# A perceiver layer on one core: the first pair's loads, its key normalisation and two other steps are rearranged

## The chip, the cores and the metric

The kernel runs on one core of one Trainium2 chip. The core has five engines with an instruction stream each: TensorE (PE in the profile, with its weight loads as PEld), VectorE (DVE), ScalarE (ACT), GpSimd (POOL) and SyncE (SP). An engine works its stream off in order. Transfers are issued by instructions in the streams of SP, ACT or POOL. The metric is the device time of one execution in microseconds (us); three executions of the kernel before gave 618.97, 621.19 and 622.3, with a median of 621.19.

## The reference

The inputs are 32 batches of latents `x` (64 x 128), of a context (1601 x 128) and of a mask over the context, which is true for the last 0 to 400 positions of a batch. One layer is computed:

```
ln  = layernorm(layernorm(x)) * g_l + b_l             # latents, 64 rows of a batch
xn  = layernorm(ctx) * g_x + b_x                      # context
q   = ln @ Wq;   k, v = split(concat(xn, ln) @ Wkv)   # 16 heads of 64
out = softmax(mask(q k^T)) v                          # a context position counts where its mask is true
x   = x + layernorm(out @ Wout) * g_o + b_o
x   = x + self_attention(layernorm(x))                # 16 heads of 8, a distance term in the scores
x   = x + quantised_ffn(layernorm(x))                 # 128 -> 352 -> 128, fake quantisation to 8 bits
```

Only those last positions count, so a batch is worked with between 72 and 464 keys, its 64 latents among them.

## The kernel before

The batches are ranked by how many context positions they need; `order` holds the ranking and `CAPS` the number of positions that each rank may need. Batches are worked in 16 pairs (`PAIRS`): the two halves of the 128 partitions are the latents of the two batches. The first pair is small: ranks 31 and 17, with 8 and 192 context positions, in one tile and two tiles of 128 partitions.

**Weights.** Queries and keys are never formed by themselves. `a_sb` holds Wq Wk^T per head (made by `turn_weight`, which transposes four 128 x 128 blocks on TensorE and copies the bank out, and by `head_products`, four matmuls a bank, evacuated on ScalarE at line 287). So the queries of a pair are `lnT` times `a_sb` (`queries`, lines 801 and 805) and the keys are the normalised context itself, transposed (`keys_T`, lines 787 and 791). `b_sb` holds Wv Wout per head in the same way, and is made inside the main part by `late_constants`.

**Two parts with a branch between.** The prologue loads the mask and Wq on SP and the key half of Wkv on ACT, ranks the batches on VectorE (lines 168 to 193), loads the latents of the first pair (line 207) and makes `a_sb`. Then every engine reads `arm` (line 1258) and branches (line 1312) to one of three bodies of `attention`; the first has the capacities of `CAPS`, and is the one that runs. The order inside the body's start is written by hand (`tc.manual_schedule`): on SP the loads of the first pair's context and mask (`load`, lines 670 to 689), the value half of Wkv and Wout (lines 1224 and 1225), then the latents, context and mask of the second pair; on the other engines `latents(0)`, `latents_T(0)`, `measure` and `prepare` for the two batches, `queries` in four quarters with `keys_T` between.

**Normalising.** `latents` takes mean and variance with bn_stats and bn_aggr on VectorE, the power -0.5 on POOL (`rstd_of`, line 703), and then three VectorE steps: line 951 (subtract the mean, times rstd), 710 (times g), 711 (plus b). For the context, `measure` does the statistics (lines 729, 730, 699, 703), and `prepare` a small `shift` on VectorE (739), one ScalarE instruction a tile (743), two VectorE steps for g and b (237, 238), a copy of the latents into the key tile on POOL (748) and the mask terms on POOL (754).

**The main loop.** Then 128 steps (16 pairs, 8 steps of two heads each). In each step `logits` does the score matmul (833), a VectorE scan that adds the mask terms and finds the lowest value (836) and the exponential on ScalarE (841); one to four steps later the probabilities are transposed (881, 890, 896) and multiplied with the keys (916, 927), scaled by VectorE (933), and projected (961). The work of other pairs is put between by a table of steps: statistics and keys of pair t+1, loads of pair t+2, projection, self attention and FFN of the pairs before. Within the stretch between scheduling barriers the framework's scheduler may reorder an engine's instructions, so the written order is not all. In the body's first steps, `late_constants(0)` (transposes of the value weights, lines 256 and 257) stands at step 1, and products of `b_sb` at steps 2 and 3.

## Time and profile before

| what | us |
|---|---|
| median of three executions (618.97 to 622.3) | 621.19 |
| the profiled execution | 618.87 |
| its span, from the first instruction to the last | 617.2 |
| PE busy in the span | 583.2 |
| DVE, ACT, POOL busy | 444.8, 409.2, 130.4 |
| branch reached: `arm` written on VectorE | 11.47 |
| last evacuation of `a_sb` on ScalarE ends | 14.69 |
| transposed latents `lnT` ready | 17.42 |
| first score matmul starts | 25.49 |

The span is counted from the first instruction; the 1.67 us between the span and the profiled time lie around it. Four views of the profile carry what follows. The page gives busy time by engine. The table of stretches gives busy time and the clock that was granted to TensorE. The timeline lists instructions in order of time, merged where equal ones follow each other, with start, duration, engine, line, tiles, shape, and in brackets how long the engine was idle before and what it waited for. The view of one source line also shows instructions of an engine's sequencer (a name that ends in q): branches, register loads, and waits.

### The profile page before, as it was taken

What the parts mean: (1) busy time and instruction counts of PE and PEld (TensorE: products, weight loads), DVE (VectorE), ACT (ScalarE), POOL (GpSimd) and SP (SyncE); (2) the same over time, 40 slices, a digit from 0 to 9 for tenths busy, and PEclk for the clock granted to TensorE, in tenths of its full rate; (3) what the DMA queues carried; (4) which work ended last, traced back from release to release, by engine and by line L of the source; (5) the groups of instructions that cost most, each with busy time, mean ns of one, the idle gap of its engine ahead of it and who ended that gap; (6) DMA issues with size and microseconds to landing.
All of it is one profiled execution on the core that took longest, in us unless ns stands there. A gap on an engine that the chain in (4) does not pass through costs nothing. (4 is left out here: it accounts for less than half of the span.)

```text
span 617.2 us, 14248 instructions
## 1 busy us (share of the span) xinstructions
PE 583.2 (94%) x4758; PEld 470.9 (76%) x4758; DVE 444.8 (72%) x1674; ACT 409.2 (66%) x1107; POOL 130.4 (21%) x320
## 2 busy tenths in 40 slices
PE   4799899999999999899999989999999999999993
PEld 4687768868896878788787878778788979777473
DVE  5578566777869676787867587786858694778983
ACT  3587476667667665676856666675767686685692
POOL 2431120424132341212120130312021211010102
PEclk9899999999999999999999999999999999999997
DMA  4433312021222112031311213011312311110002
GB/s 101 108 67 87 92 19 59 25 62 22 53 42 49 40 18 64 20 71 27 63 22 40 44 34 67 27 53 20 53 36 40 46 36 36 35 35 20 0 21 55
DMA packets 39285, 27.93 MB, mean 45 GB/s; under 512 B 18223, under 2 KB 30515, under 8 KB 39203
## 3 DMA queue, kind: packets, MB, share of 16 engines
q1 hardware_dynamic: 38755, 26.14, 20.3%
q8 instruction: 40, 0.66, 0.5%
q10 hardware_dynamic: 224, 0.56, 0.3%
q14 instruction: 42, 0.34, 0.3%
q0 software_dynamic: 224, 0.23, 0.2%
HBM read 25.73 MB, written 1.18 MB: 44 GB/s over the span
## 5 line engine op out<-in xcount | busy, mean ns | idle before, releaser
L841 ACT ACTIVATE s<-s,low 128x464 f32<-128x464 f32 (+22 forms) x256 | 133.5, 523 | 87.0 <-DVE low L836 69.5
L833 PE MATMUL bank_s<-xT,qT 128*128 128x464 f32 (+22 forms) x512 | 147.2, 406 | 4.7 <-DVE low L836 4.4
L916 PE MATMUL bank_m<-pT,xn 128*128 128x256 f32 (+10 forms) x560 | 145.0, 384 | 0.0
L916 PEld LDWEIGHTS bank_m<-pT,xn 128*128 128x128 f32 (+10 forms) x560 | 104.4, 191 | 43.1 <-issue 22.6
L703 POOL TENSOR_TENSOR rstd<-rstd,mhalf 128x1 f32<-128x1 f32 (+3 forms) x96 | 59.2, 623 | 329.5 <-DVE rstd L699 322.3
L836 DVE CUSTOM_DVE_ANT_0 s<-bank_s,ad 128x464 f32<-128x464 f32 (+22 forms) x256 | 107.3, 432 | 11.2 <-PE bank_s L833 10.3
L833 PEld LDWEIGHTS bank_s<-xT,qT 128*128 128x128 f32 x512 | 77.9, 193 | 13.4 <-DVE low L836 8.0
L933 DVE TENSOR_TENSOR oT<-bank_m,rden 128x256 f32<-128x256 f32 x128 | 77.2, 614 | 7.4 <-PE bank_m L927 2.7
L801 PE MATMUL bank_m<-lnT,a_sb 128*128 128x128 f32 x512 | 69.2, 280 | 4.5 <-DVE o L973 2.7
L901 ACT COPY pT<-bank_t 128x384 f32<-128x384 f32 (+1 forms) x128 | 60.1, 500 | 13.9 <-PE bank_t L896 9.9
L801 PEld LDWEIGHTS bank_m<-lnT,a_sb 128*128 128x128 f32 x512 | 63.7, 195 | 6.1 <-DVE o L973 3.2
L890 PE MATMUL bank_t<-ident,s 128*128 128x128 f32 x376 | 61.1, 275 | 0.9 <-DVE p L1047 0.9
L961 PE MATMUL bank_m<-b_sb,oT 128*128 128x128 f32 x512 | 60.9, 276 | 0.3 <-DVE oT L933 0.3
L961 PEld LDWEIGHTS bank_m<-b_sb,oT 128*128 128x128 f32 x512 | 59.0, 192 | 1.5 <-DVE oT L933 1.3
L805 ACT COPY qT<-bank_m 128x512 f32<-128x512 f32 x64 | 37.4, 584 | 33.4 <-PE bank_m L801 33.4
L890 PEld LDWEIGHTS bank_t<-ident,s 128*128 128x128 f32 x376 | 45.4, 141 | 12.4 <-ACT s L841 3.4
L841 ACT ACTIVATION_READ_ACCUMULATOR s<-s,low 128x1 f32 x256 | 48.6, 190 | 0.0
L743 ACT ACTIVATE xn<-xn,shift,rstd 128x128 f32<-128x128 f32 x76 | 34.5, 492 | 16.8 <-DVE shift L739 16.8
L882 ACT COPY pT<-bank_t 128x256 f32<-128x256 f32 (+1 forms) x64 | 28.5, 471 | 6.8 <-PE bank_t L881 6.6
L754 POOL TENSOR_SCALAR ad<-mask 128x64 f32<-128x64 uint8 (+16 forms) x67 | 18.4, 275 | 63.2 <-DMA mask<-in_mask_BxS_bk_dram 57.5
L729 DVE BATCH_NORM_STATS2 st<-xn 128x6 f32<-128x128 f32 x76 | 20.0, 278 | 15.3 <-DMA xn<-in_ctx_dram 15.1
L881 PE MATMUL bank_t<-ident,s 128*128 128x128 f32 x192 | 29.6, 275 | 0.0
(192 smaller groups left out, 858.2 us busy)
## 6 DMA issues: line engine op xcount, KB each, us to landing
rden<-line SPq DMA_DIRECT2D x64, 256.0 KB
xn<-in_ctx_dram SPq DMA_DIRECT2D x37, 32.0 KB
x<-in_x_dram SPq DMA_DIRECT2D x32, 32.0 KB
line<-den SPq DMA_DIRECT2D x64, 2.0 KB
out_dram<-y SPq DMA_DIRECT2D x24, 32.0 KB
wk_sb<-in_L_xattn_Wkv_dram ACTq DMA_DIRECT2D x1, 512.0 KB
wq_sb<-in_L_xattn_Wq_dram SPq DMA_DIRECT2D x1, 512.0 KB
wv_sb<-in_L_xattn_Wkv_dram SPq DMA_DIRECT2D x1, 512.0 KB
```

The lines of the kernel that those rows point to most:

```text
L703: nc.gpsimd.tensor_tensor(rstd, rstd, mhalf[:, :n], ALU.pow)
L743: nc.scalar.activation(xn[:, n, :], xn[:, n, :], AF.Identity, bias=shift[:, n : n + 1], scale=rstd[:, n : n + 1],)
L801: nc.tensor.matmul(pm[:, j * P : (j + 1) * P], lhsT=a_sb[:, h4 + j, :], rhs=lnTs[t], start=True, stop=True,)
L805: nc.scalar.copy(qTs[t][:, :, h4 : h4 + 4, :].rearrange("p u h i -> p h u i"), pm.rearrange("p (h u i) -> p h u i", h=4, u=2),)
L833: nc.tensor.matmul(ps[:, : e - k], lhsT=w, rhs=xTs[t, u][:, lo + k : lo + e], start=True, stop=True)
L836: nc.vector.tensor_tensor_reduce(out=s[:, k:e], in0=ps[:, : e - k], in1=addends[u][t % NA][:, lo + k : lo + e], scale=-1.0, scalar=3e38 if ...
L841: nc.scalar.activation(s, s, AF.Exp, bias=low[:, len(pieces) - 1 :], scale=-1.0, accum_out=den[:, odd * n_us + i : odd * n_us + i + 1],)
L890: nc.tensor.transpose(bt[:, j - n, :], s[:, lo : lo + P], ident)
L901: nc.scalar.copy(pT[:, n:e, odd, :], bt[:, : e - n, :])
L916: nc.tensor.matmul(po[:, : 2 * P], lhsT=xns[u][t % NX][:k, n, :], rhs=pT[:k, n].rearrange("p o c -> p (o c)"), start=(n == 0), stop=(n == ...
L933: nc.vector.tensor_tensor(oTs[t][:, 2 * c : 2 * c + 4, v, :].rearrange("p (o h) i -> p o h i", o=2), open_.pop(v)[:, : 2 * P].rearrange("p ...
L961: nc.tensor.matmul(pm[:, :D], lhsT=oT[:, h].rearrange("p u i -> p (u i)"), rhs=b_sb[:, h, :], start=(h == 0), stop=(h == H - 1),)
```

## The change

- The first pair's loads move ahead of the branch. The context and mask go to tiles of their own (`xn_0`, `mask_0`), cleared on POOL. The loads of the first batch (latents, context, mask: three transfers) are issued by SP, those of the second (latents, two of context, mask: four) by ACT, between its copies of `wqT` and its evacuations of `a_sb`. All transposes of Wq and Wk now stand ahead of the products.
- The load of the value weights goes to SP before any of these, that of Wout to SP ahead of the branch, after the latents of the second pair, which move there too.
- In the body, the transposes of the value weights (`late_constants(0)`) move from step 1 to just behind `latents_T(0)`, ahead of the queries. Both `measure` and both `prepare` come before the keys' transposes, which come behind all four quarters of the queries.
- The first pair's context is normalised on VectorE alone: per tile, (x - mean) * g and then times rstd plus b. The copy of the latents stands ahead of it.
- `latents` of every pair uses the same two steps in place of three.
- `ones` moves to a pool that is freed early, and a 128 x 128 tile `one`, set by POOL, takes its place in small matmuls of the FFN.

```
+    one = const.tile([P, P], FP, name="one")
+    nc.gpsimd.memset(one, 1.0)
...
-    first_pair = [batch(0, u) for u in range(2)]
-    for u in range(2):
-        load_x(0, u, first_pair[u])
...
-    for g in range(2):
-        turn_weight(wqT, wq_sb, 4 * g, nc.scalar.copy)
-        turn_weight(wkT, wk_sb, 4 * g, nc.vector.tensor_copy)
-        head_products(a_sb, wqT, wkT, E ** -0.5, g)
+    def load_first(u, eng):
+        b = batch(0, u, engine=(mybir.EngineType.SP, mybir.EngineType.Activation)[u])
+        load_x(0, u, b, eng)
...
+        eng.dma_start(out=xn[lo : lo + f, 0, :], in_=rows[S2 - n : S2 - n + f])
+        if nt:
+            eng.dma_start(
+                out=xn[:pr, 1 : 1 + nt, :],
+                in_=rows[S2 - nt * pr :].rearrange("(p n) d -> p n d", n=nt),
+            )
+        eng.dma_start(
+            out=m, in_=mask[bass.ds(b, 1)].rearrange("b s -> (b s)")[S2 - n :].partition_broadcast(P)
+        )
...
+        nc.gpsimd.memset(xn_0[u], 0.0)
+    load_first(0, nc.sync)
+    with tc.manual_schedule(engines={mybir.EngineType.Activation}):
+        turn_weight(wqT, wq_sb, 0, nc.scalar.copy)
+        turn_weight(wkT, wk_sb, 0, nc.vector.tensor_copy)
+        turn_weight(wqT, wq_sb, 4, nc.scalar.copy)
+        turn_weight(wkT, wk_sb, 4, nc.vector.tensor_copy)
+        load_first(1, nc.scalar)
+        for g in range(2):
+            head_products(a_sb, wqT, wkT, E ** -0.5, g)
+    nc.sync.dma_start(out=wv_sb, in_=heads[:, 1])
+    for u in range(2):
+        load_x(1, u, batch(1, u))
+    nc.sync.dma_start(out=wout_sb, in_=wout.rearrange("(c f) d -> f c d", f=P))
...
+        def affine1(dst, src, mean, rstd, g, b):
+
+            nc.vector.scalar_tensor_tensor(dst, src, mean, g, ALU.subtract, ALU.mult)
+            nc.vector.scalar_tensor_tensor(dst, dst, rstd, b, ALU.mult, ALU.add)
...
-            norm1(n, x1[:, t, :], twice=True)
-            nc.vector.tensor_tensor(n, n, gl_r, ALU.mult)
-            nc.vector.tensor_tensor(n, n, bl_r, ALU.add)
+            affine1(n, x1[:, t, :], *moments(x1[:, t, :], twice=True), gl_r, bl_r)
...
+            if t == 0:
+
+                nc.gpsimd.tensor_copy(xn[lat[u], 0, :], lns[t][lat[u]])
+                for n in range(n_all):
+                    on = slice(0, P) if n else tok[u]
+                    affine1(xn[on, n, :], xn[on, n, :], mv[on, n, 0:1], rstd[on, n : n + 1], gx_r[on], bx_r[on])
...
-            nc.sync.dma_start(out=wv_sb, in_=heads[:, 1])
-            nc.sync.dma_start(out=wout_sb, in_=wout.rearrange("(c f) d -> f c d", f=P))
             if narrow:
                 for u in range(2):
                     load(1, u)
             latents(0)
             latents_T(0)
+            late_constants(0)
             measure(0, 0)
-            queries(0, 0)
-            prepare(0, 0)
             if narrow:
                 measure(0, 1)
+            queries(0, 0)
             queries(0, 4)
-            keys_T(0, 0)
             queries(0, 8)
+            prepare(0, 0)
             if narrow:
                 prepare(0, 1)
             queries(0, 12)
+            keys_T(0, 0)
             if narrow:
                 keys_T(0, 1)
```

More of the change, by code (lines that the diff above doesn't have):

```diff
@@ L124, in late_loads @@
             nc.sync.dma_start(out=r, in_=w.partition_broadcast(P))
-    ones = const.tile([P, QW], FP, name="ones")
+    ones = look.tile([P, QW], FP, name="ones")
     nc.vector.memset(ones, 1.0)
@@ L185, in perceiver_layer @@
             )
-    nc.vector.tensor_copy(order, rank)
-    nc.vector.tensor_single_scalar(order, order, B - 1, op=ALU.bitwise_and)
+    with tc.manual_schedule(engines={mybir.EngineType.DVE}):
+        nc.vector.tensor_copy(order, rank)
+        nc.vector.tensor_single_scalar(order, order, B - 1, op=ALU.bitwise_and)
     over = look.tile([1, B], FP, name="over")
@@ L204, in perceiver_layer, with load_x @@
     x1 = const.tile([P, NP, D], FP, name="x1")
-    def load_x(t, u, b):
-        nc.sync.dma_start(
+    def load_x(t, u, b, eng=nc.sync):
+        eng.dma_start(
             out=x1[u * SL : (u + 1) * SL, t, :],
@@ L287, in head_products @@
             nc.scalar.mul(view, pm, scale)
-    for g in range(2):
-        turn_weight(wqT, wq_sb, 4 * g, nc.scalar.copy)
-        turn_weight(wkT, wk_sb, 4 * g, nc.vector.tensor_copy)
-        head_products(a_sb, wqT, wkT, E ** -0.5, g)
+    xn_0, mask_0 = [], []
+    def load_first(u, eng):
+        b = batch(0, u, engine=(mybir.EngineType.SP, mybir.EngineType.Activation)[u])
+        load_x(0, u, b, eng)
+        f, nt, pr, rest = CAPS[PAIRS[0][u]]
+        n = f + nt * pr
+        xn, m = xn_0[u], mask_0[u]
+        rows = context[bass.ds(b, 1)].rearrange("b s d -> (b s) d")
+        lo = SL * (1 - u)
+        eng.dma_start(out=xn[lo : lo + f, 0, :], in_=rows[S2 - n : S2 - n + f])
[4 more added lines that the diff above has]
+            )
+        eng.dma_start(
+            out=m, in_=mask[bass.ds(b, 1)].rearrange("b s -> (b s)")[S2 - n :].partition_broadcast(P)
+        )
+    for u in range(2):
+        f, nt, pr, rest = CAPS[PAIRS[0][u]]
+        assert not rest
+        xn_0.append(prep.tile([P, 1 + nt, D], FP, name=f"xn_0{u}"))
+        mask_0.append(prep.tile([P, f + nt * pr], U8, name=f"mask_0{u}"))
+        nc.gpsimd.memset(xn_0[u], 0.0)
[9 more added lines that the diff above has]
+    nc.sync.dma_start(out=wv_sb, in_=heads[:, 1])
+    for u in range(2):
+        load_x(1, u, batch(1, u))
+    nc.sync.dma_start(out=wout_sb, in_=wout.rearrange("(c f) d -> f c d", f=P))
     blk4 = const.tile([P, 4], FP, name="blk4")
@@ L441, in act_scale @@
             nc.vector.tensor_reduce(mx[:1], bt[:1, :P], AX.X, ALU.max)
-            nc.tensor.matmul(bt[:, P : P + 1], lhsT=ones[:1, :P], rhs=mx[:1], start=True, stop=True)
+            nc.tensor.matmul(bt[:, P : P + 1], lhsT=one[:1, :P], rhs=mx[:1], start=True, stop=True)
             nc.vector.tensor_copy(full, bt[:, P : P + 1])
@@ L465, in missed @@
             pm = bank_m()
-            nc.tensor.matmul(pm[:1, : n_x + n_h], lhsT=ones[:, :1], rhs=far, start=True, stop=True)
+            nc.tensor.matmul(pm[:1, : n_x + n_h], lhsT=one[:, :1], rhs=far, start=True, stop=True)
             count = self.ff.tile([1, 1], FP, name="count")
@@ L658, in attention, with keys_of @@
         masks, lns, lnTs, xTs, qTs, oTs, probs, pTs, sums = {}, {}, {}, {}, {}, {}, {}, {}, {}
+        def keys_of(t, u):
+            return xn_0[u] if ahead and t == 0 else xns[u][t % NX]
         def load(t, u):
+            if ahead and t == 0:
+                masks[t, u] = mask_0[u]
+                return
             r = xns[u][t % NX]
@@ L663, in load @@
             first = S2 - cap(t, u)
-            b = first_pair[u] if t == 0 else batch(t, u)
-            if t and narrow:
+            b = batch(t, u)
+            if t > 1 and narrow:
                 load_x(t, u, b)
@@ L724, in measure @@
             n_all = shape(t, u)[2]
-            xn = xns[u][t % NX][:, :n_all]
+            xn = keys_of(t, u)[:, :n_all]
             st = small.tile([P, n_max[u], 6], FP, tag=f"st{name}{u}", name="st")
@@ L735, in prepare @@
             nt, rest, n_all, sk = shape(t, u)
-            xn = xns[u][t % NX][:, :n_all]
+            xn = keys_of(t, u)[:, :n_all]
             mv, rstd = moments_of.pop((t, u))
-            shift = small.tile([P, n_max[u]], FP, tag=f"shift{name}{u}", name="shift")
-            nc.vector.scalar_tensor_tensor(
-                shift[:, :n_all], mv[:, :n_all, 0], -1.0, rstd, ALU.mult, ALU.mult
-            )
-            for n in range(n_all):
+            if t == 0:
[3 more added lines that the diff above has]
+                    affine1(xn[on, n, :], xn[on, n, :], mv[on, n, 0:1], rstd[on, n : n + 1], gx_r[on], bx_r[on])
+            shift = small.tile([P, n_max[u]], FP, tag=f"shift{name}{u}", name="shift")
+            if t:
+                nc.vector.scalar_tensor_tensor(
+                    shift[:, :n_all], mv[:, :n_all, 0], -1.0, rstd, ALU.mult, ALU.mult
+                )
+            for n in range(n_all if t else 0):
                 nc.scalar.activation(
@@ L746, in prepare @@
                 )
-            affine(xn, n_all, gx_r, bx_r, nc.vector)
-            nc.gpsimd.tensor_copy(xn[lat[u], 0, :], lns[t][lat[u]])
+            if t:
+                affine(xn, n_all, gx_r, bx_r, nc.vector)
+                nc.gpsimd.tensor_copy(xn[lat[u], 0, :], lns[t][lat[u]])
             m, ad = masks.pop((t, u)), addends[u][t % NA]
@@ L772, in keys_T @@
             nt, rest, n_all, sk = shape(t, u)
-            xn = xns[u][t % NX]
+            xn = keys_of(t, u)
             if (t, u) not in xTs:
@@ L916, in attend @@
                 nc.tensor.matmul(
-                    po[:, : 2 * P], lhsT=xns[u][t % NX][:k, n, :],
+                    po[:, : 2 * P], lhsT=keys_of(t, u)[:k, n, :],
                     rhs=pT[:k, n].rearrange("p o c -> p (o c)"),
@@ L1179, in attention @@
                     if t + 1 < NP:
-                        at(s0 + 2, lambda t, u: load_x(t, u, batch(t, u)), t + 1, u)
+                        if t:
+                            at(s0 + 2, lambda t, u: load_x(t, u, batch(t, u)), t + 1, u)
                     if (t, u) != (NP - 1, 1):
@@ L1186, in attention @@
                         at(s0 + 8 * u + 6, keys_T, *nxt)
-        for k in range(4):
-            at((1,2,3,12)[k], late_constants, k)
+        for k, i in ((1, 2), (2, 3), (3, 12)):
+            at(i, late_constants, k)
         at(1, clear_values)
```

## The prediction

> **What bounds the kernel now.** I read the page first, then the table of stretches.

> ```profile
> PE 583.2 (94%) x4758; PEld 470.9 (76%) x4758; DVE 444.8 (72%) x1674; ACT 409.2 (66%) x1107; POOL 130.4 (21%) x320
> ```
> ```profile
> 0.00:25.50 25.50, 13.70 (x86) 12.08 (x87) 12.03 (x50) 8.86 (x17) 6.05 (x51) 0.93 0.45 115
> 35.00:45.00 10.00, 10.00 (x76) 9.27 (x75) 6.92 (x28) 8.45 (x25) 2.75 (x7) 1.00 0.33 69
> 200.00:300.00 100.00, 98.16 (x829) 79.89 (x828) 74.22 (x288) 67.49 (x188) 26.34 (x52) 1.00 0.20 41
> ```

> A row gives a stretch, its length, the busy time of PE, PEld, DVE, ACT and POOL, then PE's granted clock. From 25.5 us PE is nearly always busy and is the bound; before that it is busy for 13.70 of 25.50 us. So time comes from two places: an earlier first score matmul, and PE work taken out of the full stretch. VectorE work saved later is worth only what it saves PE in waits.

> Then the timeline of the start, for the chain that sets the first score matmul:

> ```profile
> 13.84 0.29 DVE L943 BATCH_NORM_STATS2 st<-x 128x6 f32<-128x128 f32 x1 [2.37 <-DMA x<-in_x_dram]
> ...
> 15.94 0.42 DVE L711 TENSOR_TENSOR ln<-ln,bl_r 128x128 f32<-128x128 f32 x1
> 16.64 0.52 SPq L670 DMA_DIRECT2D xn<-in_ctx_dram  x1
> 16.66 0.14 PEld L256 LDWEIGHTS bank_t<-ident,ln 128*128 128x128 f32 x1 [2.80 <-issue]
> ...
> 17.15 0.27 ACT L257 COPY lnT<-bank_t 128x128 f32<-128x128 f32 x1 [2.46 <-PE bank_t L256]
> 17.43 0.36 SPq L673 DMA_DIRECT2D xn<-in_ctx_dram  x1
> ...
> 18.05 0.33 SPq L689 DMA_DIRECT2D mask<-in_mask_BxS_bk_dram  x1
> ...
> 20.32 0.28 DVE L729 BATCH_NORM_STATS2 st<-xn 128x6 f32<-128x128 f32 x1
> ...
> 23.05 0.88 ACT L743 ACTIVATE xn<-xn,shift,rstd 128x128 f32<-128x128 f32 x2
> ...
> 24.42 0.42 DVE L238 TENSOR_TENSOR xn<-xn,bx_r 128x256 f32<-128x256 f32 x1
> 24.92 0.14 PEld L787 LDWEIGHTS bank_t<-ident,xn 128*128 128x128 f32 x1 [1.69 <-ACT qT L805]
> ...
> 25.49 0.34 PE L833 MATMUL bank_s<-xT,qT 128*128 128x72 f32 x2
> ```

> The latents give `lnT` at 17.42; the keys of the second batch end last, at 24.84, behind statistics, power, ScalarE and two VectorE steps in turn. The queries' matmuls (line 801) end at 23.42 and are not last. PE's clock in the rows of 1 us is 0.70 in 18 to 19, 0.50 from 19 to 21, 0.60 in 21 to 22: half speed from some 18.4 to 21.4, behind the idle time from 14.06.

> Last, the sequencers at the branch, by the view of its lines:

> ```profile
> L1258 ACTq TENSOR_LOAD <-arm x1: 478/478/478, 14.1 to 14.1; - x1
> ```
> ```profile
> L1261 ACTq BRANCH_PREFETCH_HINT  x1: 54/54/54, 15.3 to 15.3; - x1
> ```

> ScalarE reads `arm` when it has sent its last `a_sb` evacuation off, and is in the body 1.25 us later. TensorE had its hint at 14.2, so it waited for `ln`.

> **The change, part by part.** Sums are against the profiled execution: 618.87 us, span 617.2 and 1.67 around it. It is the lowest of what is shown, 2.32 under the median; I carry the difference over to the median.

> *Loads on ACT.* ACT's sequencer is free when `order` is (9.99; SP's first load of latents is issued at 10.73). The latents took SP 0.92 for the first issue and 0.48 for later ones; the same context and mask transfers ran from 16.64 to 18.38, 1.74 us. So ACT issues from 10.75 to 11.67, and with a gap of 0.23 to 13.65. Queued behind are the four `a_sb` evacuations: they start at 13.65 in place of 12.25 and end 2.44 later, 16.09. TensorE's fourth group waits for the first of them (14.25, done by 15.1). ACT's branch: the fourth evacuation is sent off at 15.5, plus 1.25 gives 16.75. Bounds: the longest issue of a mask in the start is 1.29 (at 15.08), so +1.0; with short issues throughout, -0.45. I take 1.74, from the same transfers.

> *Latents.* The second load of latents starts at 10.75 on ACT, not after the first on SP. Before, it began near 11.8 and VectorE got it at 13.84, so now at 13.0 or a little later (Wv, 512 KB, is now ahead of it; 0 to 0.6). Statistics take 0.7 to 13.9; POOL's clearing runs to 14.37 as before, so the power is there at 15.02. The first step (0.35 by line 973, of the same form) runs beside it; the second ends at 15.4, against 16.36. Transposed at 15.75 to 16.05. Now ACT is last: the copy of `lnT` runs from 16.8 to 17.07, so **0.35 us** are gained there, not 0.96.

> *Queries.* While ACT is awaited, TensorE does the eight value transposes from 16.05 (0.11 each at full clock, 0.21 at half, by line 256 at 25 to 28 us and at 8.77): no cost. Then 32 query records, 0.111 each at full clock (line 801, 8 in 0.89 us): 17.1 to 20.65, the bank copies (0.59) beside them. ACT's two value copies (1.18) end before the first bank is full.

> *Keys.* Loads issued at 11.9 to 13.3 have landed when VectorE takes them at 15.4. Statistics of three tiles, 0.65 and 1.1, to 17.15; POOL's power 0.70, to 17.95; six steps of 0.35 (half of them before it), last at 19.4. The transposes are due at 20.65, so VectorE is hidden by 1.2 us. The three ScalarE steps (0.50 + 0.88) and `shift` go.

> *First scores.* Key transposes 0.45 behind 20.65; ACT's last query copy to 21.3, key copy 0.22; score matmul at 21.55, against 25.49. **Minus 3.9.**

> *Value transposes out of the full stretch:* 8 x 0.11 = **0.9** (bounds 0, if ScalarE paces these steps, and 1.4, by their records 0.39 + 0.60 + 0.38).

> *Steady state.* Sixteen VectorE steps of 0.29 to 0.43 go. The instruction order of VectorE changes in each pair only around `xl` and `ln`; in one place, near 76 us, a scan (836) now stands ahead of a step that waited 0.41 us for POOL:

> ```profile
> 76.68 2.75 PE L833 MATMUL bank_s<-xT,qT 128*128 128x284 f32 x4 [0.90 <-DVE low L836]
> ```
> I take **0.7** here (0.41 and the step's 0.35 less rounding). Bounds: a gain of 2.2 if the half clock right behind it (0.61 and 0.54 in 76 to 80, some 1.5 us lost) goes too; a loss of 1.5 if such a dip comes at another place, as every later step shifts.

> *At nothing:* SP issues the second pair's loads from about 17.6 to 24.7 (before, 20.07 to 28.50); the first `den` transfer, due at 30.12 - 5 = 25.1, stands behind them, so 0 to 0.6. Wout is issued near 15.3, used after 21. POOL's three new memsets are done by 4 us, under the mask's load (5.42).

> Sum: -3.9 - 0.9 - 0.7 = -5.5. The profiled execution would take 613.4, and the median 621.19 - 5.5 = **615.7 us**.

> **Rules weighed.** ACT's instruction packet came at 15.8, after its hint at 15.3; POOL's first body instruction started at 12.85, right after its hint at 12.7 and before any instruction packet (the first at 13.2). [...]

> TensorE lost half its clock at 18.4 after 2.6 idle us, and near 76 after gaps of 1.31 and 0.90. After the change its gaps are 0.9 (13.35 to 14.25) and 0.65 (15.1 to 15.75), shorter than either, so I take no dip. [...]

> **Rivals.**
> *Hidden or paid back.* ACT's issues take 1.0 longer and the clock dips again at 17 to 21 (1.5): first scores at 24.05, and with 0.9 for the transposes and nothing in the steady state the gain is 2.3: 618.9. For it: the 1.29 row, the dip near 76. Against: the same transfers took 1.74.
> *More than summed.* The dips at 18 and 76 both go and the transposes give 1.4: 3.9 + 1.4 + 2.2 = 7.5: 613.7.
> *Slower.* The first step of `ln` now stands ahead of `xl` on VectorE, and a scan stands behind both, in 14 pairs. If each pair makes PE wait, it is slower by over 3.1 us once the loss passes (4.8 + 3.1) / 14 = 0.56 us a pair; at 0.7, 621.19 - 4.8 + 9.8 = 626.2. Against it: PE waited for VectorE scans only six times, 4.4 us in all, and a pair has 0.36 us less VectorE work.
> *The copy of `lnT` isn't earlier* (no gain at the branch): then all rests on the keys; 0.35 less, inside the first.

> **How the numbers follow.** About 0.5% (3.1 us; 618.1 to 624.3) is what a measurement can tell from no change. My forecast has 0.55, more than summed 0.15, hidden 0.22, slower 0.08. Faster by over 0.5%: 0.53 of the forecast, all of the second and 0.04 of the third, 0.72; the same: 0.02 + 0.18 = 0.20; slower 0.08. The range runs from 612.5 (the second, less 1.2 for how far the three executions scatter about their median) to 620.0 (the first rival plus 1.1); 0.12 lie outside.

> **What would show it.** Right: first score matmul near 21.5, `lnT` copy waiting on ACT's own issue near 16.8, the first pair's keys normalised by 20, clock 1.00 through 22 us, no idle time over 0.3 at the scan near 72. Wrong: ACT's four issues taking over 3 us; scores not before 24; new PE waits for scans, one a pair; the second pair's statistics waiting for loads.

## The result

The changed kernel takes **612.5 us** (median of six executions, 611.37 to 613.9), against 620.66 for the kernel before on the same chip (618.97 to 622.3): 0.9865 of it, with a 95% interval of 0.984 to 0.9891. A second set of six gave 611.88 against 620.47, 0.9867 (0.9831 to 0.9903). So it is 8.2 to 8.6 us faster by these medians. The forecast was a gain of 5.5 us and 615.7; the result lies at the lower end of the range (612.5 to 620.0), the second set 0.6 us below it, and nearest to the rival "more than summed" (613.7).

The profiled execution took 611.37 us, with a span of 609.2. First busy time by engine on its page, then the stretches that answer to those shown before (start and end, length, then busy time and instructions of PE, PEld, DVE, ACT and POOL, then the clock granted to TensorE).

```profile
PE 578.8 (95%) x4758; PEld 469.4 (77%) x4758; DVE 440.0 (72%) x1658; ACT 408.3 (67%) x1104; POOL 129.7 (21%) x323
```
```profile
0.00:22.40 22.40, 13.53 (x96) 12.26 (x96) 12.56 (x51) 8.69 (x17) 8.71 (x58) 1.00 0.46 132
35.00:45.00 10.00, 9.04 (x56) 7.12 (x54) 6.30 (x26) 6.91 (x22) 3.14 (x13) 1.00 0.48 80
200.00:300.00 100.00, 97.96 (x831) 80.08 (x830) 75.48 (x285) 68.47 (x191) 22.92 (x48) 1.00 0.20 41
```

TensorE is still the bound. What precedes the first score matmul is 3.1 us shorter, at a clock of 1.00 instead of 0.93. The timeline of the start:

```profile
13.14 0.29 DVE L996 BATCH_NORM_STATS2 st<-x 128x6 f32<-128x128 f32 x1 [1.81 <-DMA x<-in_x_dram]
13.27 1.57 ACT L286 ACTIVATE a_sb<-bank_m 128x512 f32<-128x512 f32 x3 [2.95 <-POOL xn L682]
...
13.92 1.16 PE L278 MATMUL bank_m<-wkT,wqT 64*128 64x128 f32 x8 [0.44 <-ACT a_sb L286]
...
15.18 0.35 DVE L750 SCALAR_TENSOR_TENSOR ln<-x,mv,gl_r 128x128 f32<-128x128 f32 x1 [1.34 <-DMA x<-in_x_dram]
15.27 0.12 POOL L459 MEMSET mxs<- 128x15 f32 x1 [1.38 <-ACT a_sb L286]
15.44 0.57 POOL L745 TENSOR_TENSOR rstd<-rstd,mhalf 128x1 f32<-128x1 f32 x1
...
16.05 0.55 DVE L751 SCALAR_TENSOR_TENSOR ln<-ln,rstd,bl_r 128x128 f32<-128x128 f32 x1 [0.51 <-POOL rstd L745]
...
16.99 1.04 PE L255 MATMUL bank_t<-ident,wv_sb 128*128 128x128 f32 x8
...
17.31 0.27 ACT L256 COPY lnT<-bank_t 128x128 f32<-128x128 f32 x1 [1.60 <-DVE rstd L741]
...
17.86 3.74 PE L854 MATMUL bank_m<-lnT,a_sb 128*128 128x128 f32 x32
...
20.37 0.35 DVE L751 SCALAR_TENSOR_TENSOR xn<-xn,rstd,bx_r 128x128 f32<-128x128 f32 x1
...
22.39 0.44 PE L886 MATMUL bank_s<-xT,qT 128*128 128x72 f32 x2
```

`lnT` is ready at 17.58, later than before (17.42) and than forecast (17.07). The latents' statistics are there at 13.83, yet the first step of `ln` starts at 15.18. The profile names the load of `x`, which had been taken at 13.14; so it was another wait. The last matmul of the eight that begin at 13.92 ends at 15.08, and both the step and POOL's clearing of `mxs` start just behind it. What carries this on to `lnT` is the clearing: POOL takes up the power behind it, at 15.44, and the second step of `ln` waits 0.51 us for the power after the first has ended. The gain comes after that: the queries (32 matmuls of line 854) take 3.74 us, where the kernel before needed from 17.47 to 23.42 with its clock at half for 3.4 of them, and the keys are ready at 20.72 without ScalarE.

### The profile page after: what moved, and what is told of

It is laid out like the page before. It is cut to its first block, busy times and chain, and to the rows that moved or that the text cites. A ratio compares the mean times of both kernels' runs of the same rounds, so it can differ in the third digit from the quotient of the medians.

```text
span 609.2 us, 14242 instructions
## 1 busy us (share of the span) xinstructions
PE 578.8 (95%) x4758; PEld 469.4 (77%) x4758; DVE 440.0 (72%) x1658; ACT 408.3 (67%) x1104; POOL 129.7 (21%) x323
## 3 DMA queue, kind: packets, MB, share of 16 engines
q1 hardware_dynamic: 38269, 25.97, 21.3%
HBM read 25.71 MB, written 1.18 MB: 44 GB/s over the span
## 5 line engine op out<-in xcount | busy, mean ns | idle before, releaser
L889 DVE CUSTOM_DVE_ANT_0 s<-bank_s,ad 128x464 f32<-128x464 f32 (+22 forms) x256 | 107.3, 432 | 16.2 <-PE bank_s L886 14.8
L886 PEld LDWEIGHTS bank_s<-xT,qT 128*128 128x128 f32 x512 | 77.6, 192 | 14.2 <-DVE low L889 8.6
L854 PE MATMUL bank_m<-lnT,a_sb 128*128 128x128 f32 x512 | 67.5, 276 | 3.9 <-DVE o L1026 2.7
L954 ACT COPY pT<-bank_t 128x384 f32<-128x384 f32 (+1 forms) x128 | 60.0, 500 | 14.1 <-PE bank_t L949 9.9
L854 PEld LDWEIGHTS bank_m<-lnT,a_sb 128*128 128x128 f32 x512 | 62.4, 192 | 5.2 <-DVE o L1026 3.2
L943 PE MATMUL bank_t<-ident,s 128*128 128x128 f32 x376 | 61.1, 275 | 0.9 <-DVE p L1100 0.9
L943 PEld LDWEIGHTS bank_t<-ident,s 128*128 128x128 f32 x376 | 45.4, 140 | 12.4 <-issue 3.7
L795 ACT ACTIVATE xn<-xn,shift,rstd 128x128 f32<-128x128 f32 x73 | 32.9, 488 | 16.1 <-DVE shift L791 16.1
L807 POOL TENSOR_SCALAR ad<-mask 128x64 f32<-128x64 uint8 (+16 forms) x67 | 18.4, 275 | 63.3 <-DMA mask<-in_mask_BxS_bk_dram 56.8
L774 DVE BATCH_NORM_STATS2 st<-xn 128x6 f32<-128x128 f32 x76 | 20.0, 278 | 15.2 <-DMA xn<-in_ctx_dram 15.1
```

What stands on the lines that cost most here:

```text
L854: nc.tensor.matmul(pm[:, j * P : (j + 1) * P], lhsT=a_sb[:, h4 + j, :], rhs=lnTs[t], start=True, stop=True,)
L886: nc.tensor.matmul(ps[:, : e - k], lhsT=w, rhs=xTs[t, u][:, lo + k : lo + e], start=True, stop=True)
L889: nc.vector.tensor_tensor_reduce(out=s[:, k:e], in0=ps[:, : e - k], in1=addends[u][t % NA][:, lo + k : lo + e], scale=-1.0, scalar=3e38 if ...
L943: nc.tensor.transpose(bt[:, j - n, :], s[:, lo : lo + P], ident)
L954: nc.scalar.copy(pT[:, n:e, odd, :], bt[:, : e - n, :])
```

## The experiments

### One memory, two users: the wait in the start

The theory: `ln` and `mxs` lie in memory that `wqT` and `wkT` gave back, and the products still read those. Here the two weights get memory that is first written much later:

```
-    wqT = look.tile([P, 8, D], FP, name="wqT")
-    wkT = look.tile([P, 8, D], FP, name="wkT")
+    x3 = const.tile([P, NP, D], FP, name="x3")
+    wqT, wkT = x3[:, :8, :], x3[:, 8:, :]
```

> The changed kernel, with the transposed weights wqT and wkT kept in the memory of x3 (which is first written near 115 us), in place of memory that the body's tiles take over. Theory C (the first step of ln, at 15.18 in the profile of the changed kernel, waited 1.34 us for the last product, because ln lies on memory that the products still read): the step starts at 13.9, the copy of lnT at 16.2 in place of 17.3, the first score matmul near 21.1 in place of 22.4, 1.0 to 1.3 us off the whole. Rival (the wait is for the latents' load or ScalarE): no change of the step's start, time within 0.3 of the changed kernel.

Measured: 609.97 us, 0.9848 (0.9806 to 0.9891). The timeline of this kernel (one line less in the file, so 749 is 750 above):

```profile
13.83 0.34 DVE L749 SCALAR_TENSOR_TENSOR ln<-x,mv,gl_r 128x128 f32<-128x128 f32 x1
...
14.16 0.12 POOL L458 MEMSET mxs<- 128x15 f32 x1
14.34 0.57 POOL L744 TENSOR_TENSOR rstd<-rstd,mhalf 128x1 f32<-128x1 f32 x1
...
14.94 0.55 DVE L750 SCALAR_TENSOR_TENSOR ln<-ln,rstd,bl_r 128x128 f32<-128x128 f32 x1 [0.76 <-POOL rstd L744]
...
16.46 0.27 ACT L256 COPY lnT<-bank_t 128x128 f32<-128x128 f32 x1 [0.56 <-PE bank_t L255]
...
21.41 0.44 PE L885 MATMUL bank_s<-xT,qT 128*128 128x72 f32 x2
```

The wait of 1.34 is gone, POOL clears `mxs` at 14.16 and not at 15.27, `ln` is ready at 15.49 (forecast for the changed kernel: 15.4) and the first score matmul is at 21.41 (forecast: 21.55). So the reuse of memory is what the prediction had not seen, and it cost 0.98 us in this pair of profiles. The profile of the kernel with keys on ScalarE, told below, has the old memory, and there the same wait is put down to the product itself:

```profile
15.29 0.35 DVE L750 SCALAR_TENSOR_TENSOR ln<-x,mv,gl_r 128x128 f32<-128x128 f32 x1 [1.41 <-PE bank_m L278]
```

A second set beside a further kernel (told below):

> The changed kernel with wqT and wkT in memory of their own, unchanged from its first run (0.9848 of the kernel before). Expected 0.983 to 0.987 again, the first score matmul within 0.3 of 21.41, or 1 to 1.6 later where the clock falls at the start; if the first run was chance, 0.987 or more, as the changed kernel.

Measured: 609.78 us, 0.9827 (0.9789 to 0.9865). This is the fastest version, about 2 us under the changed kernel by the medians; the intervals of the two overlap. Its first score matmul was at 23.02 in this profile, though `lnT` was copied at 16.63, near the 16.46 above: the clock was at half from 16.6 to 20.0.

### Unchanged, once more

> The changed kernel once more, so that the next three can be set against it on the same chip. Expected: 0.984 to 0.989 of the kernel before, first score matmul at 22.4 us, clock at full speed through 70 to 80 us in most executions.

Measured: 611.88 us, as told. Its profile copies `lnT` at 17.27, near the 17.31 of the first, but a clock of 0.66 from 16 to 21, and the first score matmul at 23.97, 1.6 us later. So one and the same program loses its clock at the start in some executions and not in others. This touches each reading that follows.

### The second queue

```
-        b = batch(0, u, engine=(mybir.EngineType.SP, mybir.EngineType.Activation)[u])
+        b = batch(0, u)
...
-        load_first(1, nc.scalar)
+        load_first(1, nc.sync)
```

> The changed kernel, with the second batch's loads on SP behind the first's (four issues of ACT move to SP). If ACT's issues hold back the evacuations of a_sb, the last product and with it the memory of wqT and wkT: evacuations from 12.2 in place of 13.27, last product matmul near 14.0 in place of 15.07, ln ready near 15.6, first score matmul 21.4 to 21.8 in place of 22.39, and some 1 us is won, less what the second pair's loads lose (SP is free some 2.6 us later). If the first pair's loads are the limit instead: the last load of the second batch's context lands near 17, its keys are ready after 21, first scores at 22.4 or later, and the time is the changed kernel's or up to 1 us above it.

Measured: 615.9 us, 0.9942 (0.9919 to 0.9965): by the ratios, (0.9942 - 0.9866) x 620, 4.7 us of the gain are lost. The timeline:

```profile
12.48 1.69 ACT L286 ACTIVATE a_sb<-bank_m 128x512 f32<-128x512 f32 x3 [2.07 <-PE bank_m L278]
...
13.19 0.48 SPq L210 DMA_DIRECT2D x<-in_x_dram  x1
...
15.50 0.29 DVE L996 BATCH_NORM_STATS2 st<-x 128x6 f32<-128x128 f32 x1 [4.08 <-DMA x<-in_x_dram]
...
17.69 0.30 PE L255 MATMUL bank_t<-ident,ln 128*128 128x128 f32 x1 [3.41 <-DVE st L774]
...
24.86 0.44 PE L886 MATMUL bank_s<-xT,qT 128*128 128x72 f32 x2
```

The evacuations do start at 12.48 and the memory comes free 0.8 us earlier (the last product ends at 14.28), as the first theory had it. But the second batch's latents are issued as the fourth of the first pair's loads, at 13.19, and land at 15.5. TensorE idles 3.41 us, the clock is at half from 18.9 to 22.3, and the first scores come 2.5 us later than in the changed kernel. The first pair's steps are 1.2 us longer as well (20.27 from its first scan to the next pair's, against 19.08); why was not looked into. The second theory was right on its cause (the first pair's loads), but placed it at the keys and priced it at 0 to 1 us; it is the latents, and the clock behind them. ACT's four issues are worth more than they cost.

### Keys of the first pair on ScalarE

The `if t == 0` branches of `prepare` are taken out, so the first pair goes the way of the others; its place in the written order stays.

> The changed kernel, with the first pair's keys normalised as in the other pairs (shift, ScalarE, then two VectorE steps over the whole tile). If the two-step form on VectorE carries the start: the ScalarE steps (0.50 + 0.88) start after the power, among the query copies (0.59 each), the last keys are ready at 21.5 to 22.3 in place of 20.72, first scores near 23.3, +0.9 us. If the queries hide the keys, as the prediction had it with 1.2 us to spare: first scores at 22.4 and no difference.

Measured: 619.54 us, 0.9998 (0.9976 to 1.002): the whole gain is gone. The timeline, and the table of stretches for the stretch behind it:

```profile
18.91 5.60 PE L854 MATMUL bank_m<-lnT,a_sb 128*128 128x128 f32 x32
...
23.66 0.58 ACT L858 COPY qT<-bank_m 128x512 f32<-128x512 f32 x1 [0.49 <-PE bank_m L854]
24.14 0.50 ACT L795 ACTIVATE xn<-xn,shift,rstd 128x128 f32<-128x128 f32 x1
...
25.39 0.88 ACT L795 ACTIVATE xn<-xn,shift,rstd 128x128 f32<-128x128 f32 x2 [0.76 <-DVE shift L791]
...
25.77 0.28 PE L840 MATMUL bank_t<-ident,xn 72*128 72x72 f32 x1 [1.26 <-POOL xn L801]
...
27.86 0.34 PE L886 MATMUL bank_s<-xT,qT 128*128 128x72 f32 x2
```
```profile
16.00:22.00 6.00, 5.03 (x24) 5.06 (x25) 2.06 (x10) 2.02 (x4) 1.81 (x4) 0.50 0.39 114
22.00:28.00 6.00, 3.40 (x24) 2.90 (x23) 1.71 (x6) 3.03 (x7) 0.99 (x5) 0.93 0.19 43
28.00:34.00 6.00, 6.00 (x28) 4.92 (x27) 2.63 (x15) 3.31 (x13) 4.62 (x13) 0.64 0.00 0
34.00:40.00 6.00, 5.81 (x22) 4.85 (x23) 3.09 (x22) 3.50 (x12) 0.87 (x1) 0.51 0.24 56
```

Neither theory held in its size. The power is ready at 19.1, but ScalarE's steps stand behind the third query copy in its queue and start at 24.14. TensorE then waits 1.26 and 1.24 us for keys, and its clock falls to half a second time, from 29.6 to 39.9. The first fall, from 16.0 to 22.8, lengthened the queries (5.60 us, against 3.74), and with them the wait for the third copy. In twelve executions the mean clock was 0.979 to 0.986, so this was no accident of one. The run tests ScalarE's steps in the new order, not in the old one. Its loss and the 4.7 us of the second queue can't be added up as parts of one gain: each run also changes what the rest waits for.

### Value transposes back at step 1

```
-        for k, i in ((1, 2), (2, 3), (3, 12)):
+        for k, i in ((0, 1), (1, 2), (2, 3), (3, 12)):
...
-            late_constants(0)
```

> The changed kernel, with the eight transposes of the value weights back at step 1 of the body (Wv still loaded early). By the prediction's term they cost 8 x 0.11 = 0.9 us in the full stretch (0 to 1.4), and the first score matmul stays at 22.4: about 612.8. Rival: without them TensorE idles from the transposes of ln (17.2) to the copy of lnT (17.6) and longer ahead of that, the clock falls to half in the queries as in the kernel before, the first scores come 1 to 1.5 us later: 613.9 to 614.3. Second rival: ScalarE paces step 1, and it costs nothing.

Measured: 611.91 us, 0.9866 (0.984 to 0.9893), the changed kernel's own ratio. The first pair's steps last 19.29 us from its first scan to the next pair's, against 19.08 and 19.09, so 0.2 us of the 0.9 are to be seen; a wait of 0.35 us at the scan near 27 is gone in exchange. The clock fell to half from 18.6 to 22.0 in this profile, as in one of the two of the changed kernel. Over its five executions the clock takes 6.2 us, against 4.8 in the changed kernel (table below), which is the way of the first rival, but the time shows no loss. The place of these transposes is worth nothing that can be measured in the time.

### Two steps for the latents

First the three steps in pairs 1 to 15 of the changed kernel:

```
-            affine1(n, x1[:, t, :], *moments(x1[:, t, :], twice=True), gl_r, bl_r)
+            if t == 0:
+                affine1(n, x1[:, t, :], *moments(x1[:, t, :], twice=True), gl_r, bl_r)
+            else:
+                norm1(n, x1[:, t, :], twice=True)
+                nc.vector.tensor_tensor(n, n, gl_r, ALU.mult)
+                nc.vector.tensor_tensor(n, n, bl_r, ALU.add)
```

> The changed kernel, with the old three VectorE steps in the latents of pairs 1 to 15; the first pair and the whole start stay as changed. Theory A (the gain has a second part in the steady state: VectorE's shorter work around the latents lets scans come earlier in every pair): first score matmul unchanged at 22.4, then 0.1 to 0.2 us lost a pair, 2 to 3 us in all over the changed kernel (ratio to before 0.990 to 0.992). Theory B (the prediction's: steady-state VectorE work is hidden by TensorE, but for one place): 0.7 us lost at most (0.987 to 0.988). A half-clock stretch near 72 us would add 1.5 to either.

Measured: 619.1 us (median of eleven executions; a twelfth took 1143.27), 0.9967 (0.994 to 0.9995), far beyond either theory. But the edit did more than it says: the scheduler put statistics of pair 1 ahead of scans of pair 0 on VectorE, TensorE idled for 2.11 us, and the clock stayed at half for ten us:

```profile
33.93 0.44 PE L891 MATMUL bank_s<-xT,qT 128*128 128x72 f32 x2 [2.11 <-DVE low L894]
```
```profile
34.00:45.00 11.00, 11.00 (x48) 9.73 (x49) 4.25 (x14) 6.50 (x18) 0.57 (x2) 0.53 0.31 73
```

So this run has no say on the two steps themselves. The other way round, the two steps alone in all pairs of the kernel before:

```
-            norm1(n, x1[:, t, :], twice=True)
-            nc.vector.tensor_tensor(n, n, gl_r, ALU.mult)
-            nc.vector.tensor_tensor(n, n, bl_r, ALU.add)
+            mean, rstd = moments(x1[:, t, :], twice=True)
+            nc.vector.scalar_tensor_tensor(n, x1[:, t, :], mean, gl_r, ALU.subtract, ALU.mult)
+            nc.vector.scalar_tensor_tensor(n, n, rstd, bl_r, ALU.mult, ALU.add)
```

> The kernel before, with only the two-step latents for all 16 pairs; its start stays. Theory A: the start gains at most 0.6 (one VectorE step less behind the power), the rest 2 to 3 us by pairs: 617 to 618 (0.9945 to 0.996). Theory B: 0.7 in one place and at most 0.6 at the start: 619.4 or more (0.998).

Measured: 616.86 us, 0.9944 (0.9921 to 0.9967). That is 3.6 us by the medians (2.0 to 4.9 by the interval), where the prediction had 0.7 for all of it. Three more runs split it, with the order of the first three pairs kept where the edit begins at pair 3 (`if t < 3:` in place of `if t == 0:`).

> The changed kernel, with the latents of pairs 3 to 15 back to three VectorE steps (pairs 0 to 2 keep two, so that the order of the first pairs stays). Three theories for the 2.3 us that the changed kernel won between pair 3 and the end of its trace. Waits: self_out (line 1159) waits for cT again in the profile, 0.49 + 0.31 + 0.28 as before, so +0.8 to +1.5 us against the changed kernel (about 613.2). Chance: the waits that differed are those for loads, which differ from execution to execution, so 0 to +0.4 and no wait for cT. On the path: every step saved counts, 13 x 0.35 = +4.5 us (about 616.6).

> The kernel before, with the latents of pairs 0 to 2 alone in two VectorE steps. Dip theory: the half clock near 76 us, behind the waits at 73 and 76, goes, and with the 0.16 us of the first pair it is 1.2 to 2.4 us faster (618.2 to 619.4). On the path: 3 x 0.35 = 1.0 us faster. Chance: the dip near 76 stays in the profile and it is 0.2 us faster at most.

> The kernel before, with the latents of pairs 3 to 15 alone in two VectorE steps. Waits theory: the waits of TensorE for cT (0.49, 0.31, 0.28) are gone, the dip near 76 stays, 0.8 to 1.5 us faster (about 619.4). Chance: no difference to the kernel before. On the path: 4.5 us faster (616). This and the run with pairs 0 to 2 should add up to the 3.6 us of the run with all pairs.

Measured: the changed kernel with three steps from pair 3, 613.93 us, 0.991 (0.9881 to 0.9939); the kernel before with two steps to pair 2, 618.32 us, 0.9979 (0.9956 to 1.0002); with two steps from pair 3, 616.85 us, 0.9975 (0.9945 to 1.0006). By the medians the last two give 0.7 and 2.1 us, together 2.8 of the 3.6; neither is clear of no change by its interval. And without the wait for memory, with three steps from pair 3:

> The kernel with wqT and wkT in memory of their own, and the latents of pairs 3 to 15 back to three VectorE steps; beside it on the same chip the same without that. The earlier runs left open whether those 13 pairs are worth the 1.1 us of the waits for cT that the profiles show, or more. Waits alone: 1.1 us slower than the kernel beside it. Waits, and also the shorter pairs 6, 9 and 10 that the profiles of all two-step runs show: 1.6 to 2.2 slower. On the path: 4.5 slower.

Measured: 611.44 us, 0.9868 (0.9828 to 0.9908), 1.7 us over the kernel beside it (609.78). So the two steps of the 13 later pairs are worth 1.7 us here by the medians, 2.1 in the kernel before (1.5 by the ratio), and 2.7 in the changed one by the ratios (0.991 against 0.9867 of some 619). The intervals are wide: that of the kernel before alone reaches from nothing to 3.4.

The profiles are sharper than the times. TensorE waits for `cT` ahead of `self_out` in all five profiles with three steps from pair 3 on, 0.48 or 0.49, 0.30 to 0.32, 0.23 to 0.28 and under 0.1 us; in the nine with two, only 0.09 to 0.11 at the first of these places is left. The timelines of the changed kernel with three steps, and of the changed kernel itself, at that place (the view prints no wait under 0.15):

```profile
184.07 0.38 PE L1164 MATMUL bank_m<-swT,cT 128*128 128x128 f32 x1 [0.48 <-DVE cT L1157]
```
```profile
181.94 0.49 PE L1159 MATMUL bank_m<-swT,cT 128*128 128x128 f32 x2
```

And pairs compared from their first scan to the next pair's, as means over all profiles without a half clock in that pair (5 with three steps, 9 with two; 8 in pair 6):

```
pair            4      6      7      8      9     10     11
three steps  31.07  37.57  30.11  36.17  37.55  30.83  36.31
two steps    30.67  37.05  30.03  36.27  36.58  30.37  36.48
```

The sum of the differences is 2.2 us. Pair 3 is left out: it scatters from 37.2 to 39.1, and its means differ by 0.5 the other way, so that the sum would be 1.7 with it. Pairs 5 and 12 to 14 agree within 0.1. It is no fixed price a pair: pairs 4, 6, 9 and 10 carry nearly all of it, and in the kernel before the four waits for `cT` stand within 0.7 us behind the ends of just these pairs. The waits for `cT` add up to about 1.0 us of the 2.2, a shorter wait of the queries for `o` in pair 9 (1.22 against 0.88 on average) another 0.3; the rest isn't traced to a wait. This bears out the theory of waits, with twice its size, against "on the path" (4.5) and "chance" (0).

The dip theory fell. The half clock near 76 us stood in one profile alone, that of the kernel before. The kernel before with two steps from pair 3 on has the same two waits there (1.21 and 0.90) and no half clock behind them. The run with two steps to pair 2 lost its clock elsewhere, from 22.0 to 39.1 and from 141.5 to 144.9.

### What the clock takes

The mean granted clock of every execution is on record, so span times (1 - clock) says about how much the lower clock took. The profiled execution of the changed kernel reads 609.2 x 0.005 = 3.0 us with a full clock up to 600 us: that is the end, from 602.6 us on, where TensorE has nearly nothing to do, and all 14 profiles have it. Means over the executions of each kernel:

| kernel | executions | span x (1 - clock), us |
|---|---|---|
| before (beside the first experiments) | 23 | 8.0 |
| changed, both sets | 12 | 4.8 |
| changed, memory of their own, both sets | 12 | 3.7 |
| two steps alone | 12 | 7.4 |
| value transposes back at step 1 | 5 | 6.2 |
| first pair all on SP | 12 | 7.0 |
| three steps from pair 1 | 11 | 8.5 |
| keys on ScalarE | 12 | 11.1 |

So about 3.2 us of the changed kernel's gain is clock, and the rest, 5 to 5.4 us, is work and waits. The kernel with keys on ScalarE loses 6.2 us more than the changed one to the clock, which is most of what it lost (8.2 by the ratios). This sum is an estimate: it reads a mean that is given to three digits (0.3 us in half its last digit), and supposes that each us at half clock costs half a us. The matmuls of line 801 in the kernel before start 0.21 us apart at a granted clock of 0.50 (18.95 to 20.02 us) and 0.11 at 1.00 (17.69 to 18.36), so it can hold only where TensorE is always busy.

## Why the prediction was off

The gain came out some 3 us larger than forecast. The step that failed most is the steady state: the two-step latents of the later pairs were put at nothing, since only TensorE's waits for scans were counted, and the runs show 2.2 us there, in part in waits for other tiles. The next is the clock, read from one profile: 1.7 us were counted, and 3.2 shown. At the start a step failed the other way: `ln` was late.

Each term of the sum beside what the runs showed. The half clock at the start (rows of 0.70, 0.50, 0.50 and 0.60, 1.7 us; it ends at 21.8, not at 21.4 as the prediction read it) is taken out of the first term and put with the clock, since it turned out to vary.

| term | forecast | shown |
|---|---|---|
| first scores, without the clock | 2.2 | 1.4 (3.1 less 1.7) |
| value transposes | 0.9 | 0.2 seen, nothing in the time |
| scan near 76 | 0.7 | 0.6 (0.90 less 0.31) |
| two steps of the latents, pairs 3 to 15 | 0 | 2.2 |
| clock | 1.7 | 3.2 |
| sum | 5.5 | 7.6 of 8.2 to 8.6 |

The terms shown come from single profiles, from means over profiles and from mean clocks, so the sum is an estimate, and 0.6 to 1.0 us of the gain has no term.

**First scores.** The evacuations (13.27 forecast as 13.65), ScalarE's branch hint at 16.1 (16.75), the landing of `x` (13.14, as forecast 13.0 or a little later) and the keys hidden behind the queries (20.72 before 21.43) were right or near. The step that failed is "POOL's clearing runs to 14.37 as before, so the power is there at 15.02", and with it "the second ends at 15.4". In the changed kernel ACT's issues push the last product to 15.08, and with it the memory that `ln` and `mxs` are to take: the clearing of `mxs` ends at 15.39, the power at 16.01, the second step at 16.60. So the forecast bound, ScalarE at 16.75, was not the one that held, and `lnT` came 0.16 later than before in place of 0.35 earlier. With memory of their own, `ln` and the first scores came within 0.15 us of the forecast, though not link by link: the copy of `lnT` waited for TensorE, not for ScalarE's issue, and `lnT` was ready at 16.73, 0.34 ahead of the forecast, while the queries took 0.2 longer.

**Keys.** "VectorE is hidden by 1.2 us" was right in kind for the changed kernel, with 0.7 to spare, but the prediction never priced what the old form would cost behind it in the new order. It costs the whole gain.

**Value transposes.** "No cost" in the start was nearly right: the queries start 0.28 us behind `lnT` (17.86 after 17.58), while the last of these transposes end, and 0.05 behind it in the kernel before. "0.9 out of the full stretch" was not. There a wait of 0.35 stands instead, and the bound of 0 that the prediction kept was the better value.

**The scan near 76** was foreseen. In the kernel before it stood behind the step that waited for POOL; in the changed kernel it stands ahead of it, and TensorE's wait of 0.90 is gone. Two waits for scans are there in its place, of 0.14 (under what the view prints) and 0.17. The kernel before, then the changed one:

```profile
75.90 0.35 DVE L976 SCALAR_TENSOR_TENSOR x<-o,rstd,x 128x128 f32<-128x128 f32 x1 [0.41 <-POOL rstd L703]
76.17 0.45 DVE L836 CUSTOM_DVE_ANT_0 s<-bank_s,ad 128x284 f32<-128x284 f32 x1
```

```profile
72.13 0.45 DVE L889 CUSTOM_DVE_ANT_0 s<-bank_s,ad 128x284 f32<-128x284 f32 x1
...
72.62 0.35 DVE L1029 SCALAR_TENSOR_TENSOR x<-o,rstd,x 128x128 f32<-128x128 f32 x1
72.64 0.75 PE L886 MATMUL bank_s<-xT,qT 128*128 128x284 f32 x2
...
73.55 0.99 PE L886 MATMUL bank_s<-xT,qT 128*128 128x432 f32 x2 [0.17 <-DVE low L889]
```

The kernel before with the two steps alone still has the wait of 0.90, so the gain belongs to the changed order at the start, not to the two steps.

**Steady state.** The prediction counted PE's waits for scans (4.4 us, six times) and let the waits for `cT` and `o` stand, though its rule was that saved VectorE work is worth what it saves PE in waits. Those waits were in the trace of before (0.49, 0.31 and 0.28 for `cT`, 1.00 and 1.69 for `o`), and on VectorE `cT` stands there behind scans, and those behind the steps of `ln` (184 to 187 us). This is the largest term that was missed.

**Clock.** The prediction took the two half clocks of one profile as the kernel's own: one to go, one to stay. They differ between executions of one program (a clock of 1.00 through 22.4 us in one profile of the changed kernel, of 0.66 from 16 to 21 us in the other), which one profile can't tell. The forecast of no dip at the start was right for the profile above and wrong for others; its gaps there are 0.44 and 1.78 us, where 0.9 and 0.65 were forecast, since the wait for memory lengthens the second.

The rivals: "more than summed" came nearest in its number, by luck. It had the dips at 18 and 76 gone for good and 1.4 us from the value transposes; the dips differ from execution to execution, and the transposes gave nothing that the time shows. "Slower" asked for a new wait a pair, and no profile shows one. "Hidden or paid back" asked for a dip at 17 to 21; it came in four of the seven profiles with this start (three steps later on, or memory of their own, among them), and the gain did not fall to 2.3, since the rest of the sum was larger. ScalarE's branch had no say in the end: with the hint at 16.1, `lnT` waited for `ln`, whose transpose ended at 17.15. The instruction packet that the prediction gives to ScalarE is at 15.9 in the trace of the kernel before, and the trace doesn't name the engine that it was for.

## What to carry to other kernels

When loads or evacuations move, look for tiles whose memory comes from a pool that is freed near by: here their first writer waited 1.34 us for the last reader of what lay there, and the profile named a load that had been taken 2.04 us before (13.14, against 15.18). Count every wait of the bounding engine that stands behind the engine you relieve, not only the commonest one. Behind 8 of 29 waits of TensorE of 1.2 to 2.6 us the clock fell to half in these profiles, 3.4 us or longer, so where the bound is TensorE, read the mean clock of many executions ahead of a dip in one.

## What the runs showed of the hardware

In the 14 profiles, TensorE waited for 1.2 to 2.6 us at 29 places between 26 and 580 us; behind 8 of them the granted clock fell to half, between the end of the wait and 2.4 us later. The other 11 falls ahead of 600 us began at the start, between 15.98 and 22.00 us.

Worked out from the rows of 1 us (twice the sum of what is missing to 1.00), these 19 falls lasted 3.40 to 3.42 us (14 of them), 6.82 and 6.84, 10.24 (two), and 17.08: within 0.02 us, 1, 2, 3 and 5 times 3.413. One of 10.24 lies in the row of 34 to 45 us shown above, at half clock with TensorE busy for 11.00 of 11.00 us.

```
wait (us)    2.58   2.46   2.37   2.17   2.00   1.98
clock after  half   full   half   full   full   half
busy share   0.25   0.48   0.35   0.66   0.43   0.42
```

So in these profiles a fall behind a wait went with the busy share of such a stretch more than with the length of the wait. What places the stretches in an execution was not shown.
